# Block 0's pass and products moved into the stretch between the steps, and the output blocks' roots taken on GpSimd as a power, with their steps three slots apart

## Chip, cores and metric

The program runs on one core of one Trainium2 chip. The metric is device time in microseconds. Engines are called PE (TensorE), DVE (VectorE), ACT (ScalarE), POOL (GpSimd) and SP (the queue of SyncE that starts most DMAs); L12 is line 12 of the kernel before the change.

## What is computed

Two layers on 2708 nodes with 256 features. The first is a graph layer with a residual and a layer norm. The second makes two propagation steps, over the normalised adjacency R and over an attention A that keeps, in each row of a softmax, the largest entries up to a mass of 0.9.

```python
x = _layernorm(x + relu(concat([x, adj @ x]) @ weight + bias))
R = adj + eye;  R = R / R.sum(-1, keepdims=True)
Z, Xf, Xa = 0, x, x
for n in range(2):
    A = top_p_attention(Xa, W1, W2, W3)      # softmax, nucleus of 0.9, renormalised
    Xf = R @ Xf
    Xa = A @ Xa
    Z = Z + Xf @ U1[n].T + Xa @ U2[n].T
h = x + Z
x = _layernorm(x + _layernorm(h) * ln_g + ln_b)
```

(`adj` is the second layer's S too. A layer norm divides by the root of the variance plus 1e-5.)

## The kernel before

The nodes are cut into 22 blocks of 128 rows, the last with 20. The first layer runs to about 285 us. Then come the two attention steps; the change touches the border between them and all of the second.

**Step 2 as a pipeline.** A loop `for per in range(NB + 2)` (L1271) has periods, each cut into six slots `g`. What is issued in a slot stands in each engine's queue in the order of the code, and every engine works its queue in that order. In period `per` four blocks are under way:

- block `per + 2` (`b_exp`): logits on PE (L507, in three parts, with one PSUM buffer), `shift` on DVE (L841, the row maximum of an excerpt), Exp on ACT (`exps2`, L844 and L848), and at the end `begin_search` on DVE (L852 to L857);
- block `per + 1` (`b_act`): a search for the threshold in whole passes over the row on ACT (`try_act`: L965, Relu with a sum; L968, Sign with a sum; small steps L971 to L981);
- blocks `per` and `per - 1`: on DVE (`vector_slots`), the one gets `last_level`, `below_level` (L1022) and `candidates` (L1029), the other `in_order` (L1038, L1041), `threshold`, `mark` (L1082) and `mask` (L1087), which sets what is dropped to zero;
- block `t_mul = per - 2`: `turn` (PE transposes four 128 x 128 blocks, L527; ACT copies them to `wT`, L530 and L533) and `products` (L564, one slot later), six groups for 22 blocks.

Blocks 0 to 2 are started ahead of the loop: their logits and Exp end beside `ya_pair` (L672 on PE, copies L675 on ACT), which makes the right side of the products. DVE searches block 0 by two passes (`try_dve`, L992), and ACT makes one more (`try_act(b0, 1, 0)`, after all of the `ya_pair`s). The spill of ACT's passes is the upper half of `tile2`, in the room of `xaT_all`, which the `ya_pair`s read.

**R's products.** R has few entries per row, so for a block m of R only the needed rows are fetched: seven indirect DMAs on POOL (`y_load`, L719), and two loads of R's values and one of own rows on SP. Eight matmul steps ("units", `r_units`, L749) make the product. `y_load` of block m + 1 is issued with the first unit of m and needs the buffer of m - 1. A table `units` says how many units a period issues: 8, 8, then 18 in periods 2 to 9, none in 10, and 16 from 11 on (two blocks of R: their first units are in slots 0 and 3). In slot 0 units stand ahead of the first `turn`, in the others behind it.

**Output blocks.** When a block has its product with A and its second with R (`arrive`, L792), it goes to `ready`. A `Final` then gets two layer norms, one a period: `load` of x1 (SP, L1176), `stats` (DVE, L1181 and L1182), `roots` (ACT, Sqrt, L1217), `over` (DVE, reciprocal L1220 and L1221), then `end` for blocks at their second norm and `middle` for those at their first: both apply the norm on ACT (L1191), `middle` also scales and adds on POOL (L1206, L1207), and `store` (SP, L1214). `final_slot` spreads them: `over`, `end` and `middle` in slot 0, `store` in 1, `load` in 2, `stats` in 3, `roots` in 5. In the last period (`tail`) the norm is applied on DVE, and after the loop `roots` and `over` are called three times more for what is left.

Of the kernel before, what the change touches and what calls it, by code (L numbers as in the profile page):

```python
# [9 lines left out]
FP = mybir.dt.float32  # L10
I32 = mybir.dt.int32
AF = mybir.ActivationFunctionType  # L12
ALU = mybir.AluOpType
# [5 lines left out]
LN_EPS = 1e-5  # L19

P = 128
# [19 lines left out]
CW, CC = 128, 7  # L41
# [107 lines left out]
def fast_path(ctx, tc, c, flags, fint, xT_d, x_d, w0_d, b0_d, w1_d, w2_d, w3_d, u1_d, u2_d, g_d, b_d):  # L149
    nc = tc.nc  # L150
# [3 lines left out]
    NW = SEG * NS  # L154
# [344 lines left out]
    def logits(s, t, i):  # L499


        p = rows(t)
        lg = ps_lg()
        cs = CHS[2 * i:2 * i + 2]
        for h, (a, b) in enumerate(cs):
            o = slice(DA * h, DA * h + DA)
            nc.tensor.matmul(lg[:p, h, :b - a], lhsT=q[o, t * P:t * P + p], rhs=keys[s][o, i, :b - a],  # L507
                             start=True, stop=True)
        a, b = cs[0][0], cs[-1][1]
        return lg.rearrange("p h n -> p (h n)")[:p, :b - a], a, b  # L510
# [151 lines left out]
    def ya_pair():  # L662


        if not y_pairs:
            return
        t0 = y_pairs.pop(0)
        pz = ps_acc().rearrange("p (s d) -> p s d", d=D)
        for s in range(2):
            p, at = rows(t0 + s), (t0 + s) * P  # L670
            for j in range(DC):
                nc.tensor.matmul(pz[:p, s, :], lhsT=xaT_all[:, j, at:at + p], rhs=c.u2[:, j, 1, :],  # L672
                                 start=j == 0, stop=j == DC - 1)
        if rows(t0 + 1) == P:
            nc.scalar.copy(ya[:, t0:t0 + 2, :], pz)  # L675
            return
        for s in range(2):
            nc.scalar.copy(ya[:rows(t0 + s), t0 + s, :], pz[:rows(t0 + s), s, :])
# [129 lines left out]
    def e2(t):  # L808
        return ring[t % 5]
# [40 lines left out]
    def begin_search(b):  # L850

        nc.vector.tensor_reduce(b.z, b.all[:b.p, :NL], AX.X, ALU.add)  # L852
        yield
        nc.vector.reciprocal(b.rz, b.z)
        nc.vector.tensor_scalar(b.nz, b.z, -1.0, None, op0=ALU.mult)
        yield
        nc.vector.tensor_scalar(b.l0, b.roots, b.roots, b.rz, op0=ALU.mult, op1=ALU.mult)  # L857

    def run_all(steps):
        for _ in steps:  # L860
            pass
# [84 lines left out]
    for t in range(3):  # L946
        exps2(blocks[t], 2, *logits(1, t, 2))
        ya_pair()
    while y_pairs:
        ya_pair()  # L950

    tile1 = big.tile([P, 2 * NW], FP, tag="x1", name="w")
    low = tile1[:, :NW]
    w = tile1[:, NW:]
    tile2 = big.tile([P, 2 * NW], FP, tag="V", name="e4")
    nc.gpsimd.memset(tile2[:, N:NW], 0.0)
    ring.append(tile2[:, :NW])
    scr = tile2[:, NW:]

    def try_act(b, k, part):  # L960


        e = e2(b.t)[:b.p, :N]
        if part == 0:
            nc.scalar.activation(scr[:b.p, :N], e, AF.Relu, bias=b.nz, scale=b.l[k], accum_out=b.relu)  # L965
            return
        if part == 1:
            nc.scalar.activation(scr[:b.p, :N], e, AF.Sign, bias=b.nz, scale=b.l[k], accum_out=b.sign)  # L968
            return
        if part == 2:  # L970
            nc.scalar.activation(b.n, b.sign, AF.Identity, bias=halfn[:b.p], scale=0.5)  # L971
            return
        nc.scalar.activation(b.u[k], b.relu, AF.Identity, bias=b.n, scale=b.rz)
        next_level(b, k)

    def next_level(b, k):
        keep, slope, down = STEPS[k]
        nc.scalar.activation(b.kept, b.l[k], AF.Copy, scale=keep + TOP_P * slope, bias=-down)
        nc.scalar.activation((b.l1, b.l2)[k], b.u[k], AF.Identity, bias=b.kept, scale=-slope)
        if k:  # L980
            nc.scalar.activation(b.few, b.l1, AF.Copy, scale=TOP_P, bias=-FEW)  # L981
# [6 lines left out]
    def try_dve(b, k):  # L988

        e = e2(b.t)[:b.p, :N]  # L990
        level(b, b.l[k])
        nc.vector.scalar_tensor_tensor(w[:b.p, :N], e, b.d, e, op0=ALU.is_ge, op1=ALU.mult, accum_out=b.m)  # L992
        nc.vector.tensor_scalar(b.u[k], b.m, b.rz, b.l[k], op0=ALU.mult, op1=ALU.mult)
        if k == 0:
            keep, slope, down = STEPS[0]
            nc.vector.tensor_scalar(b.kept, b.l0, keep + TOP_P * slope, -down, op0=ALU.mult, op1=ALU.add)
            nc.vector.scalar_tensor_tensor(b.l1, b.u0, -slope, b.kept, op0=ALU.mult, op1=ALU.add)
# [165 lines left out]
    sds = small.tile([P, 8], FP, tag="sds", name="sds", bufs=1)  # L1163
    nbs = small.tile([P, 8], FP, tag="nbs", name="nbs", bufs=1)
    nc.gpsimd.memset(mvs, 1.0)

    class Final:

# [45 lines left out]
            nc.sync.dma_start(out=out_d[t * P:t * P + p, :], in_=self.h[:p])  # L1214

    def roots(a, b):
        nc.scalar.activation(sds[:, a:b], mvs[:, a:b, 1], AF.Sqrt, bias=c.eps, scale=1.0)  # L1217

    def over(a, b):
        nc.vector.reciprocal(sds[:, a:b], sds[:, a:b])  # L1220
        nc.vector.scalar_tensor_tensor(nbs[:, a:b], mvs[:, a:b, 0], -1.0, sds[:, a:b], op0=ALU.mult, op1=ALU.mult)  # L1221

    def final_slot(i):


        if i == 2:
            while ready and len(new) < 2:
                new.append(Final(*ready.pop(0)))
                new[-1].load()
        if i == 1:  # L1230
            while done:
                done.pop().store()
        n = len(new) + len(finals)
        if i == 3:
            for k, f in enumerate(new + finals):
                f.stats(k)
        if i == 5 and n:
            roots(0, n)
        if i == 0 and n:
            over(0, n)  # L1240
            for f in finals:
                f.end()
            for f in new:
                f.middle()
            done[:] = finals
            finals[:] = new
            new.clear()

    accs = {}


    each = NB * (CC + 1)
    first = 2 * (CC + 1)
    units = {0: CC + 1, 1: CC + 1}
    rest = each - first - sum(units.values())
    units.update({p: rest * (p - 1) // 8 - rest * (p - 2) // 8 for p in range(2, 10)})
    units.update({p: each * (p - 10) // 11 - each * (p - 11) // 11 for p in range(11, 22)})
    assert first + sum(units.values()) == 2 * each

# [1 line left out]
    b0, b1, b2 = (blocks[t] for t in range(3))  # L1261
    run_all(begin_search(b0))
    try_dve(b0, 0)
    run_all(begin_search(b1))
    try_dve(b0, 1)
    run_all(begin_search(b2))
    lg = logits(1, 3, 0)
    r_units(first)
    try_act(b0, 1, 0)
    next_level(b0, 1)  # L1270
    for per in range(NB + 2):  # L1271
        if per == NB + 1:
            tail.append(True)
        n_r = units.get(per, 0)
        b_act = blocks.get(per + 1)
        t_mul = per - 2 if per > 1 else None
        if t_mul is not None:
            accs[t_mul] = ps_acc(t_mul)
        b_exp = None
        if per and per + 2 < NB:  # L1280
            b_exp = blocks[per + 2] = Block(per + 2)
        vector = vector_slots(blocks.get(per), blocks.get(per - 1), begin_search(b_exp) if b_exp else None)
        for g in range(NG):
            n = n_r * (g + 1) // NG - n_r * g // NG
            now = later.pop(0)
            later.append([])
            if g == 0:
                if b_exp:
                    shift(b_exp, lg[0])
                r_units(n)  # L1290
            if t_mul == EDGE:
                if g == 0:
                    products(0)
                    edge_product(ya, accs[EDGE], e2(EDGE))
            elif t_mul is not None:
                turn(t_mul, g, ya, accs[t_mul], e2(t_mul))
            if b_exp and g == 3:
                lg = logits(1, b_exp.t, 2)
            if g == NG - 1 and 3 < per + 3 < NB:
                lg = logits(1, per + 3, 0)  # L1300
            if g:
                r_units(n)
            if b_exp and g == 1:
                lg = logits(1, b_exp.t, 1)
            if t_mul is not None and t_mul != EDGE:
                products(1)
            if b_exp and g in (0, 1, 3):
                exps2(b_exp, (g + 1) // 2, *lg)
            if b_act:
                for k, part in {0: ((0, 0),), 1: ((0, 1), (0, 2), (0, 3)), 2: ((1, 0),), 3: ((1, 1), (1, 2), (1, 3))}.get(g, ()):  # L1310
                    try_act(b_act, k, part)
            next(vector)
            if g == 0:
                final_slot(0)
                if t_mul:
                    t = t_mul - 1
                    base = za_load(t)
                    later[0].append(lambda t=t, base=base: arrive(t, base, accs.pop(t), ras.pop(t)[:rows(t)]))
            for f in now:
                f()  # L1320
            if g and (per < NB + 1 or g < NG - 1):
                final_slot(g)
    t = EDGE
    base = za_load(t)
# [405 lines left out]
```

## Time and profile before

| | us |
|---|---|
| three runs | 1323.46, 1325.51, 1327.99 (median 1325.51) |
| profiled execution, device time | 1323.33 |
| its span, first to last instruction | 1321.6 |
| PE busy in it | 1237.4 (94%) |
| DVE busy | 1002.0 (76%) |
| ACT busy | 753.3 (57%) |
| POOL busy | 634.7 (48%) |

The profile is of one execution. Its span leaves out 1.7 us around the program. Shares of the whole span mix stages: before 285 us PE is nearly alone, afterwards all engines work at once. "Idle before" in a row tells how long an engine stood still and what ended that; idle time of an engine that others do not wait for costs nothing.

Step 2 begins with the last `ya_pair` near 754 us and ends with the span. The masks (L1087) of blocks 0 and 1 start at 777.32 and 807.62; then they come 24.17 us apart up to block 8, and from block 12 to 18 about 26.65 us apart.

### The profile page before, as it was taken

The page shows a single profiled execution, that of the slowest core. Times are in us where ns is not written, and L with a number is a line of the kernel's source. Part 1 is how long each engine was busy: PE and PEld are TensorE (multiplying, and loading weights), DVE is VectorE, ACT ScalarE, POOL GpSimd, SP SyncE. Part 2 cuts the span into 40 slices and gives each one's busy share as a digit, 9 for nine tenths or more (in the row PEclk, how much of TensorE's full clock was granted, in tenths as well). Part 3 has the DMA queues.
Part 4 walks back from the last instruction along what each step waited for, and adds up shares of the span by engine and source line. Part 5 has one row for each costly group of instructions (what it writes and reads, how often), then busy time and mean ns, then how long its engine had stood idle before and what let it go on. Part 6 is the DMA issues. An engine that isn't in the chain of part 4 may idle for free.

```text
span 1321.6 us, 18910 instructions
## 1 busy us (share of the span) xinstructions
PE 1237.4 (94%) x5764; PEld 894.5 (68%) x5764; DVE 1002.0 (76%) x3420; ACT 753.3 (57%) x1338; POOL 634.7 (48%) x594
## 2 busy tenths in 40 slices
PE   8999999979899999999999969999999989998985
PEld 6877877833477777777775647777756766666763
DVE  2545555865999998877751399898897999899996
ACT  2010111025465556566564498878888899989931
POOL 1000000005275532677554187887847767787850
PEclk9999999989899999999998979999999999999998
DMA  7455544523222210223232155556545445544541
GB/s 191 163 173 168 167 153 142 171 67 123 92 77 82 70 62 10 76 91 99 76 77 86 55 172 179 177 178 184 172 118 159 148 128 166 173 148 146 166 108 38
DMA packets 101994, 166.28 MB, mean 126 GB/s; under 512 B 17394, under 2 KB 74358, under 8 KB 101882
## 3 DMA queue, kind: packets, MB, share of 16 engines
q1 hardware_dynamic: 75596, 108.91, 25.4%
q0 software_dynamic: 20544, 51.17, 14.1%
q10 hardware_dynamic: 5742, 4.89, 1.3%
q8 instruction: 48, 0.79, 0.2%
q14 instruction: 64, 0.52, 0.1%
HBM read 130.87 MB, written 34.03 MB: 125 GB/s over the span
## 4 chain that ended last, share of the span: by engine, by line
PE 70%; ACT 15%; DVE 11%; issue 3%; DMA 0%; ACTq 0%; DVEq 0%
PE acc L564 23%; PE acc L257 16%; PE lg L507 8%; PE tr L527 6%; PE misc L749 5%; ACT e L965 4%; ACT e L844 3%; ACT e L968 2%; DVE e L1087 2%; PE acc L651 2%; PE acc L462 2%; PE misc L426 2%; PE misc L392 2%; ACT e L848 2%; PE acc L672 2%
## 5 line engine op out<-in xcount | busy, mean ns | idle before, releaser
L530 ACT COPY wT<-tr 128x512 f32<-128x512 f32 (+2 forms) x258 | 131.8, 518 | 217.6 <-PE tr L527 215.9
L564 PE MATMUL acc<-ya,wT 128*128 128x256 f32 (+1 forms) x924 | 234.9, 394 | 11.4 <-ACT wT L530 11.0
L564 PE MATMUL acc<-x,wT 128*128 128x256 f32 (+1 forms) x924 | 230.5, 388 | 0.0
L719 POOL DMA_INDIRECT yg<-v_d,ix x154 | 195.0, 1266 | 64.6 <-issue 25.1
L564 PEld LDWEIGHTS acc<-ya,wT 128*128 128x128 f32 (+1 forms) x924 | 171.4, 194 | 66.0 <-issue 23.1
L719 POOL DMA_INDIRECT yg<-yf_d,ix x154 | 190.7, 1238 | 48.3 <-issue 24.3
L564 PEld LDWEIGHTS acc<-x,wT 128*128 128x128 f32 (+1 forms) x924 | 165.2, 189 | 71.0 <-issue 37.3
L257 PE MATMUL acc<-y,adj_t 128*128 128x257 f32 (+1 forms) x924 | 208.4, 381 | 0.0
L257 PEld LDWEIGHTS acc<-y,adj_t 128*128 128x128 f32 (+1 forms) x924 | 171.8, 189 | 32.7 <-issue 8.9
L367 POOL DMA_INDIRECT adj_t<-in_adj,ix x154 | 165.6, 1076 | 51.8 <-issue 41.7
L749 PE MATMUL misc<-yg,adj_t 128*128 128x256 f32 (+1 forms) x704 | 180.6, 392 | 5.9 <-DMA yg<-yf_d,ix 4.3
L507 PE MATMUL lg<-k,q 64*128 64x512 f32 (+3 forms) x528 | 152.4, 605 | 29.7 <-ACT e L848 22.3
L749 PEld LDWEIGHTS misc<-yg,adj_t 128*128 128x128 f32 (+1 forms) x704 | 125.2, 190 | 54.3 <-issue 23.1
L527 PE MATMUL tr<-ident,e 128*128 128x128 f32 (+2 forms) x946 | 147.9, 275 | 2.5 <-DVE e L1087 2.5
L527 PEld LDWEIGHTS tr<-ident,e 128*128 128x128 f32 (+2 forms) x946 | 114.1, 140 | 41.9 <-issue 18.8
L334 POOL DMA_DIRECT2D part_d<-e x1 | 0.6, 573 | 285.3 <-DVE e L333 285.3
L439 ACT COPY x1T<-tr 128x256 f32<-128x256 f32 (+1 forms) x22 | 8.0, 364 | 186.7 <-PE tr L438 186.7
L965 ACT ACTIVATE e<-e,st 128x2708 f32<-128x2708 f32 (+1 forms) x43 | 113.5, 2640 | 0.1
L968 ACT ACTIVATE e<-e,st 128x2708 f32<-128x2708 f32 (+1 forms) x42 | 111.0, 2642 | 0.1
L570 DVE MAX8 cand<-e 128x8 f32<-128x170 f32 (+1 forms) x352 | 87.2, 317 | 27.4 <-ACT e L514 27.4
L1029 DVE MAX8 cand<-w 128x8 f32<-128x136 f32 (+1 forms) x440 | 106.1, 285 | 0.0
L507 PEld LDWEIGHTS lg<-k,q 64*128 64x128 f32 (+1 forms) x528 | 39.5, 184 | 63.5 <-ACT e L848 30.1
(239 smaller groups left out, 1780.8 us busy)
## 6 DMA issues: line engine op xcount, KB each, us to landing
adj_t<-in_adj SPq DMA_DIRECT2D x44, 704.0 KB
adj_t<-adjc_d SPq DMA_DIRECT2D x44, 448.0 KB
adjc_d<-adj_t SPq DMA_DIRECT2D x22, 256.0 KB
base<-za_d SPq DMA_DIRECT2D x41, 128.0 KB
adjc_d<-adj_t SPq DMA_DIRECT2D x22, 192.0 KB
xt<-in_x ACTq DMA_DIRECT2D x21, 128.0 KB
x_d<-x SPq DMA_DIRECT2D x21, 128.0 KB
x1b_d<-xb SPq DMA_DIRECT2D x21, 128.0 KB
```

The costliest lines, as they stand in the source:

```text
L257: nc.tensor.matmul(acc[:p, :n], lhsT=halves[k // KH][:kw, k % KH, :p], rhs=y[:kw, k, :n], start=k == 0, stop=stop and k == NB - 1)
L367: nc.gpsimd.indirect_dma_start(out=a[:CW, i, :], out_offset=None, in_=adj_rows, in_offset=bass.IndirectOffsetOnAxis(ap=ix[:CW, m, i:i + 1] ...
L507: nc.tensor.matmul(lg[:p, h, :b - a], lhsT=q[o, t * P:t * P + p], rhs=keys[s][o, i, :b - a], start=True, stop=True)
L527: nc.tensor.transpose(tr[:kw, k % 4, :p], e[:p, k * P:k * P + kw], ident[:p, :p])
L530: nc.scalar.copy(wT[:, :full, :p], tr[:, :full, :p])
L564: nc.tensor.matmul(acc[:p, :D], lhsT=wT[:kw, k % 4, :p], rhs=y[:kw, k, :], start=k == 0, stop=k == NB - 1)
L570: nc.vector.max(dst[:p, i * 8:(i + 1) * 8], src[:p, i * step:i * step + w])
L719: nc.gpsimd.indirect_dma_start(out=y[:CW, i, :], out_offset=None, in_=rows_d, in_offset=bass.IndirectOffsetOnAxis(ap=ix[:CW, m, i:i + 1], ...
L749: nc.tensor.matmul(acc[:p, :D], lhsT=a[:kw, k, :p], rhs=y[:kw, k, :], start=k == 0, stop=k == CC)
L965: nc.scalar.activation(scr[:b.p, :N], e, AF.Relu, bias=b.nz, scale=b.l[k], accum_out=b.relu)
L968: nc.scalar.activation(scr[:b.p, :N], e, AF.Sign, bias=b.nz, scale=b.l[k], accum_out=b.sign)
L1029: nc.vector.max(b.cand[:p, 8 * i:8 * i + 8], low[:p, SEG2 * i:SEG2 * (i + 1)])
```

## The change

It has two parts.

*Block 0.* ACT's pass over block 0 is issued after the third of the `ya_pair`s that follow the Exps, ahead of the remaining ones, and spills into `low` (the lower half of the tile whose upper half is `w`) until `tile2` is there. `next_level(b0, 1)` follows DVE's second pass. Block 0 is transposed and multiplied in slots 4 and 5 of period 1, three groups in each, and no longer in period 2. Period 2 issues 20 units of R, periods 3 to 9 share the other 124 (17 or 18 each).

*Output blocks.* `roots` runs on GpSimd, as an addition of 1e-5 and a power of -0.5, and `over` loses the reciprocal. `over`, `end` and `middle` move from slot 0 to slot 2, `store` and `load` to slot 3, `stats` from slot 3 to slot 5, ahead of `roots`. In the last period `roots` is left to the calls after the loop.

```diff
     for t in range(3):
         exps2(blocks[t], 2, *logits(1, t, 2))
         ya_pair()
-    while y_pairs:
-        ya_pair()
...
-    tile2 = big.tile([P, 2 * NW], FP, tag="V", name="e4")
-    nc.gpsimd.memset(tile2[:, N:NW], 0.0)
-    ring.append(tile2[:, :NW])
-    scr = tile2[:, NW:]
+    spill_room = [low]
...
+        scr = spill_room[0]
...
+    power = small.tile([P, 8], FP, tag="power", name="power", bufs=1)
+    nc.gpsimd.memset(power, -0.5)
...
     def roots(a, b):
-        nc.scalar.activation(sds[:, a:b], mvs[:, a:b, 1], AF.Sqrt, bias=c.eps, scale=1.0)
+        nc.gpsimd.tensor_scalar(sds[:, a:b], mvs[:, a:b, 1], LN_EPS, None, op0=ALU.add)
+        nc.gpsimd.tensor_tensor(sds[:, a:b], sds[:, a:b], power[:, a:b], op=ALU.pow)
 
     def over(a, b):
-        nc.vector.reciprocal(sds[:, a:b], sds[:, a:b])
         nc.vector.scalar_tensor_tensor(nbs[:, a:b], mvs[:, a:b, 0], -1.0, sds[:, a:b], op0=ALU.mult, op1=ALU.mult)
 
     def final_slot(i):
-        if i == 2:
-            while ready and len(new) < 2:
-                new.append(Final(*ready.pop(0)))
-                new[-1].load()
-        if i == 1:
-            while done:
-                done.pop().store()
         n = len(new) + len(finals)
-        if i == 3:
-            for k, f in enumerate(new + finals):
-                f.stats(k)
-        if i == 5 and n:
-            roots(0, n)
-        if i == 0 and n:
+        if i == 2 and n:
             over(0, n)
             for f in finals:
                 f.end()
...
+        if i == 3:
+            while done:
+                done.pop().store()
+            while ready and len(new) < 2:
+                new.append(Final(*ready.pop(0)))
+                new[-1].load()
+        if i == 5:
+            for k, f in enumerate(new + finals):
+                f.stats(k)
+            if n and not tail:
+                roots(0, n)
...
-    units = {0: CC + 1, 1: CC + 1}
+    units = {0: CC + 1, 1: CC + 1, 2: 20}
...
-    units.update({p: rest * (p - 1) // 8 - rest * (p - 2) // 8 for p in range(2, 10)})
+    units.update({p: rest * (p - 2) // 7 - rest * (p - 3) // 7 for p in range(3, 10)})
...
     try_dve(b0, 0)
+    try_act(b0, 1, 0)
+    while y_pairs:
+        ya_pair()
     run_all(begin_search(b1))
     try_dve(b0, 1)
+    next_level(b0, 1)
     run_all(begin_search(b2))
+    tile2 = big.tile([P, 2 * NW], FP, tag="V", name="e4")
+    nc.gpsimd.memset(tile2[:, N:NW], 0.0)
+    ring.append(tile2[:, :NW])
+    spill_room[0] = tile2[:, NW:]
     lg = logits(1, 3, 0)
     r_units(first)
-    try_act(b0, 1, 0)
-    next_level(b0, 1)
...
-        t_mul = per - 2 if per > 1 else None
+        t_mul = 0 if per == 1 else per - 2 if per > 2 else None
...
-            elif t_mul is not None:
+            elif t_mul:
                 turn(t_mul, g, ya, accs[t_mul], e2(t_mul))
             if b_exp and g == 3:
                 lg = logits(1, b_exp.t, 2)
+            if t_mul == 0 and g > 3:
+                for i in range(3):
+                    turn(0, 3 * (g - 4) + i, ya, accs[0], e2(0))
+                    products(1)
             if g == NG - 1 and 3 < per + 3 < NB:
                 lg = logits(1, per + 3, 0)
             if g:
                 r_units(n)
...
-            if t_mul is not None and t_mul != EDGE:
+            if t_mul and t_mul != EDGE:
                 products(1)
...
             if g == 0:
-                final_slot(0)
                 if t_mul:
                     t = t_mul - 1
                     base = za_load(t)
...
-            if g and (per < NB + 1 or g < NG - 1):
+            if g:
                 final_slot(g)
```

## The prediction, made before the change was built

> **What bounds the kernel now.** I read the stretches first, engine by engine, then the timelines of two places, and last the groups and DMA issues for prices. After the window's length each row of stretches has the busy time of PE, PEld, DVE, ACT and POOL, the granted TensorE clock and the DMA share.
>
> ```profile
> 776.00:800.00 24.00, 17.05 (x69) 11.44 (x70) 23.69 (x83) 21.43 (x32) 19.49 (x15) 0.86 0.43 134
> 800.00:824.00 24.00, 23.69 (x115) 17.84 (x114) 23.19 (x89) 19.75 (x34) 19.06 (x17) 1.00 0.64 195
> 1160.85:1187.50 26.65, 23.80 (x112) 16.97 (x110) 24.25 (x87) 24.85 (x41) 21.04 (x18) 1.00 0.50 158
> ```
>
> Three regimes. Between the steps (776 to 800) DVE and ACT are full and PE has 7 us spare. From period 2 to 9 PE is full (23.69 of 24); a period takes 24.17 us, the spacing of the masks (L1087). From period 13 on, where finished output blocks are normalised too, a period takes 26.65 us and ACT is fullest. Here the chain of waits passes through ACT's searches, the mask and the output norms.
>
> Between the steps:
>
> ```profile
> 784.68 2.08 PE L507 MATMUL lg<-k,q 64*128 64x512 f32 x4 [5.17 <-ACT e L844]
> 789.38 0.28 DVE L841 TENSOR_REDUCE nmax<-lg 128x1 f32<-128x128 f32 x1
> 807.62 3.04 DVE L1087 SCALAR_TENSOR_TENSOR e<-w,st,e 128x2720 f32<-128x2720 f32 x1
> 814.29 0.60 PE L527 MATMUL tr<-ident,e 128*128 128x128 f32 x4
> ```
>
> Period 2 of DVE and ACT begins with L841, which needs the logits L507 of block 4. The mask of block 1 comes 18.2 us later and ends at 810.66; its first transposes are at 814.29, when PE is free. So period 2 has 3.6 us in hand on DVE and none on PE.
>
> In the late regime:
>
> ```profile
> 1101.09 3.04 DVE L1087 SCALAR_TENSOR_TENSOR e<-w,st,e 128x2720 f32<-128x2720 f32 x1
> 1101.57 3.37 POOL L719 DMA_INDIRECT yg<-v_d,ix  x1 [0.30 <-PE tr L527]
> 1104.45 1.28 ACT L1217 ACT_TABLE_LOAD   x1
> 1106.01 1.03 PE L749 MATMUL misc<-yg,adj_t 128*128 128x256 f32 x4
> 1107.57 0.58 ACT L530 COPY wT<-tr 128x512 f32<-128x512 f32 x1 [1.52 <-PE tr L527]
> 1108.16 1.28 ACT L844 ACT_TABLE_LOAD   x1
> 1114.60 1.08 ACT L1191 ACTIVATE yg<-yg,nbs,sds 128x256 f32<-128x256 f32 x2
> 1116.25 0.73 POOL L1206 TENSOR_TENSOR yg<-yg,gb 128x256 f32<-128x256 f32 x1 [1.34 <-ACT yg L1191]
> 1119.43 0.99 POOL L719 DMA_INDIRECT yg<-v_d,ix  x1
> ```
>
> Call the first copy of a period T (here 1107.57). ACT works without a gap from T to T+22.63 (end of slot 3), copies twice more, PE multiplies, does two R units and transposes, and the next T is at 26.65. The load for Exp lies in this loop; the load for Sqrt lies before ACT's wait of 1.52 us, outside it. A gather that meets a mask on DVE ends 0.81 us after the mask (1104.94) and not after 0.95.
>
> **Part 1, block 0.** ACT's pass over block 0 (L965) now starts at 754.30, after the last ya copies. It moves to the end of the third in-loop copy, 748.48 + 0.59 = 749.07, and takes 2.65 + 0.18. Three ya copies stand behind it; PE's two accumulators let the last pair begin only after the first of these (752.4), so it ends near 754.2, its copies at 754.9, the level steps (0.19 + 0.30 + 0.19) at 755.6. Block 1's pass was at 757.45, so ACT gains about 1.7 us; PE's first R units come 0.6 us later, behind which POOL's gathers wait by as much, uncritically.
>
> The products cost more. Slots 4 and 5 of period 1 now issue 22 transposes, six copies and five of six product groups, and these stand on PE's queue **ahead of the logits for block 4**. The copies are behind ACT's slot 3, which ends at 788.5, then at 786.8. Five groups at 2.17 us each (spacing of transposes 991.37 to 993.54), one R unit 0.5, the logits 1.06: 786.8 + 0.6 + 10.85 + 0.5 + 1.06 = 799.8. The clock of 0.86 says that one group runs at half rate, 3.24 us for 1.89 (row of 1288.23), so 801.1. L841 was at 789.38 and is 11.7 us late; behind it on DVE is the whole of period 2, behind that ACT's Exp. The mask starts 18.0 us after L841 (18.24, less the 0.67 that DVE waited there), lasts 3.05, and block 1's transposes come at 822.2 instead of 814.29: **7.9 us later**. PE idles meanwhile: 20 R units at 0.49 (1.46 for three) and logits fill 13 of 21 us. Two units more in period 2 leave two fewer later, -1.0. Part 1: **+6.9** (+4 if the clock is full and the 1.7 larger, +10 if the half clock returns).
>
> **Part 2, roots on GpSimd.** Removed per late period: two loads, 2 x 1.283 (groups view: 8 under L1217, 7 under L844), Sqrt 0.30, a reciprocal 0.15 on DVE. Worth on the path: only the load at L844, so ACT's loop falls from 26.65 to 25.37. The other 1.58 us widen a wait; they count only if PE came sooner. DVE does 26.65 - 2.12 (its wait for L844) - 0.15 = 24.4 us per period, so that is the floor beneath.
>
> The Trainium skill ("ScalarE: Activation LUTs", What ACT_TABLE_LOAD costs) gives 1.28 us plus a drain of 1.38 for a switch. The trace has 1.283 and the next instruction 0.02 us on (1104.45 + 1.28, then Sqrt at 1105.75). With the drain, seven periods would give 9.7 us more; I go by the row.
>
> Added on POOL: an add and a power on 128 x 4. Neither is in the trace. Bounds: 0.11 (memset of 128 x 16) and 1.16 (L369, 128 x 128); the add is near L358 (128 x 7, 0.26), for the power I take 0.5. Before POOL's next gathers that is 0.8, between 0.2 and 2.3.
>
> Moved: over, end and middle to slot 2, stores and loads to slot 3, statistics to slot 5. On ACT this moves four L1191 (1.97) within the loop: nothing. On DVE 2.16 us of statistics move behind the mask, covered by its wait. On SP the store waits until T+16.2 with only the next period's loads behind it: nothing. **On POOL it is not free.** L1206 ran at T+8.68. L965 of slot 2 ends at T+17.5, less 1.28 and 1.97 is T+14.2; the third L1191 releases POOL 1.65 later (1114.60 to 1116.25), T+15.87; four operations take 3.18 to the next gather: T+19.05, against T+11.86. Seven gathers queue behind, whose rows PE needs for two units *before* the next T. And the mask, at T+20.17 before, starts at T+18.89, so the first gather meets it: it ends at 18.89 + 3.04 + 0.81 = 22.74, the second starts at 23.04 and lands after the time of the DMA view:
>
> ```profile
> yg<-yf_d,ix POOLq DMA_INDIRECT x154, 3.3
> yg<-v_d,ix POOLq DMA_INDIRECT x154, 3.8
> ```
>
> That is 26.3 to 26.8. From the second R unit to the next copy are 1.13 us (four L749 in 1.03 from 1106.01, so the second unit starts near 1106.44, to 1107.57): period 27.5 to 28.0, I take **27.7, not 25.37**. Should the first gather slip in before the mask, 26.4. Seven periods (13 to 19) at +1.05: **+7.3**; ends -9.0 (25.37) and +18 (29.2: rows landing 1.5 us later, as at 768.20, where PE got one 4.3 us after its gather of 762.96 had ended).
>
> The Trainium skill ("SBUF — State Buffer", Who interferes with whom) holds that a DVE operation with two SBUF inputs takes only the shared read interface, so writing descriptors goes on. The trace has gathers of 3.37 us beside exactly such an operation. By that sentence the second gather starts at T+20.3 and lands at T+24.1, and the period would be ACT's 25.37; I go by the rows.
>
> Periods 20 to 22 are DVE's (23.4 us): 0. Tail: statistics to nbs takes 0.57 us now (1308.49 to 1309.06) and 0.94 with add and power; once or twice on the path: +0.4 (-0.3 to +3.5).
>
> **Sum.** 6.9 + 7.3 + 0.4 = +14.6. The profiled execution took 1323.33 (span 1321.6), hence 1338; the median shown is 2.2 above it, so I say 1339.
>
> **Rivals.** *ACT's loop decides the late periods*: gathers land in time, 25.37, so 6.9 - 9.0 + 0.4 = -1.7: 1323, no change. For it: the gather that starts at 1092.78 is used at 1106.01, some 9 us after landing. Against: 7.2 of these go by the move, 2.7 by the mask, 1.3 by the faster loop. *All of ACT's relief counts* (the other side): if PE reaches T sooner too, the period falls to DVE's 24.4, seven times -2.25 is -15.7, total -8.4: 1316; it decides for faster below 25.1 per period. Against: ACT waits 1.52 us at T already. *Period 2 is short*: without products it lasts PE's 13.3 us, not DVE's 21, part 1 is -1.0 and the sum +6.7: 1331. Against: DVE is 23.69 of 24 busy there. *The power is dear*: at 3 us per call POOL's cycle (14 gathers at 1.25, two held by 2.4, 3.18, 3.0) is 28.5 and `over` is late on DVE; with the wait for rows some 29.4, 1.7 more a period: 1350.
>
> **Chances.** Forecast 0.60 (own range 1330 to 1347), ACT's loop 0.15, all relief 0.10, short period 2 0.10, dear power 0.05. A change under 0.3% (4 us) can't be told from none: faster 0.11, within 0.14, slower 0.75. The range leaves out the 1316 and 1323 cases in part: 1324 to 1350.
>
> **What would show it.** Masks of blocks 0 and 1 about 43 us apart (30.3 now), L841 of block 4 near 801 with DVE idle before it; one Exp load left and none per period; late masks 27.7 apart, with L749 in slot 0 waiting for yg<-v_d and a gather of 3.4 us just behind L1207. Late masks at 25.4 and no such wait would prove part 2 wrong; a spacing of 33 there, part 1.

## The result, and the profile after

After takes **1341.45 us** (median of four executions, 1340.16 to 1345.64) where before took 1324.59 (median of four): ratio 1.0124, 95% interval 1.0105 to 1.0144. Its profiled execution has a span of 1339.1 us, before's had 1321.6. The change costs 17 us, on both sides of the middle of step 2: between the steps, and where finished blocks are normalised.

The stretches of after that answer to the three shown of before (window, length; then busy time of PE, PEld, DVE, ACT and POOL, each with its number of instructions; granted clock, DMA share, GB/s). The third is again one late period, from first copy to first copy:

```profile
776.00:800.00 24.00, 14.82 (x69) 11.42 (x68) 12.95 (x38) 15.12 (x26) 15.66 (x13) 0.79 0.35 103
800.00:824.00 24.00, 20.62 (x76) 13.19 (x75) 21.48 (x81) 17.45 (x28) 16.85 (x13) 0.86 0.52 153
1170.17:1197.41 27.24, 24.30 (x112) 16.82 (x110) 23.05 (x86) 21.89 (x37) 21.87 (x21) 1.00 0.50 153
```

In after's code the mask is L1083, the norm L1189, scale and add L1204 and L1205, add and power of the roots L1215 and L1216; L507, L530, L564, L719, L749 and L841 are where they were. Between the steps DVE was full before (23.69 of 24) and now does 12.95: it stands still for nearly half of the time. In the late period ACT fell from 24.85 to 21.89, so its relief is real and larger than the one load on its loop, and yet the period grew from 26.65 to 27.24. No engine is busy all through it; it is a chain of waits.

Between the steps, from the timeline of after (start, length, engine, line, operation, the tiles written and read; in brackets the idle time before it and what ended it):

```profile
788.79 3.60 PE L564 MATMUL acc<-ya,wT 128*128 128x256 f32 x8 [7.49 <-ACT wT L530]
801.20 1.13 PE L507 MATMUL lg<-k,q 64*128 64x512 f32 x4
802.38 0.29 DVE L841 TENSOR_REDUCE nmax<-lg 128x1 f32<-128x128 f32 x1 [13.15 <-PE lg L507]
819.88 3.04 DVE L1083 SCALAR_TENSOR_TENSOR e<-w,st,e 128x2720 f32<-128x2720 f32 x1
823.28 0.60 PE L527 MATMUL tr<-ident,e 128*128 128x128 f32 x4
```

The first product group of block 0 runs at half rate (3.60 us, 1.89 for the later ones; the granted clock is 0.54 during the first and 1.00 from 792 to 801), the logits of block 4 come only at 801.20, and DVE has waited 13.15 us for them. Block 1's mask starts 42.8 us after block 0's, 30.3 before.

A late period of after:

```profile
1174.66 0.25 POOL L1215 TENSOR_SCALAR sds<-mvs 128x4 f32<-128x4 f32 x1
1174.99 1.04 POOL L1216 TENSOR_TENSOR sds<-sds,power 128x4 f32<-128x4 f32 x1
1184.29 1.08 ACT L1189 ACTIVATE yg<-yg,nbs,sds 128x256 f32<-128x256 f32 x2
1185.94 0.72 POOL L1204 TENSOR_TENSOR yg<-yg,gb 128x256 f32<-128x256 f32 x1 [1.10 <-ACT yg L1189]
1188.94 3.04 DVE L1083 SCALAR_TENSOR_TENSOR e<-w,st,e 128x2720 f32<-128x2720 f32 x1
1189.11 3.74 POOL L719 DMA_INDIRECT yg<-v_d,ix  x1
1193.15 0.95 POOL L719 DMA_INDIRECT yg<-v_d,ix  x1 [0.31 <-issue]
1196.18 0.30 PEld L749 LDWEIGHTS misc<-yg,adj_t 128*128 128x128 f32 x2 [0.54 <-DMA yg<-v_d,ix]
1197.41 0.58 ACT L530 COPY wT<-tr 128x512 f32<-128x512 f32 x1 [5.13 <-PE tr L527]
```

Read it as a chain: ACT's norm (1184.29) releases POOL's scale and add, behind these stands the first gather, it meets the mask (1188.94) and takes 3.74 us instead of 0.95, the second gather's rows land 3.0 us after its start, PE uses them at 1196.18, then transposes, and ACT's first copy ends 5.13 us of idling.

The starts of the mask operation give the whole account. Distances of masks in us; "0 to 10" is from block 0's mask to block 10's, "late" the mean of the six distances from 12 to 18, "end" from the last mask to the end of the span. The last six rows are of experiments below: four that ran where no other waits disturb them, and two (with figures in brackets) of which only the part from block 10 on is compared:

| kernel | 0 to 10 | 11 to 12 | late | 18 to 19 | 19 to 20 | 20 to 21 | end |
|---|---|---|---|---|---|---|---|
| before | 248.1 | 25.69 | 26.64 | 23.46 | 23.37 | 15.66 | 24.8 |
| after | 255.2 | 24.28 | 27.28 | 24.22 | 27.71 | 16.47 | 27.1 |
| e11_after_here | 255.2 | 24.28 | 27.15 | 24.22 | 27.82 | 17.51 | 25.5 |
| e12_block0_again | 255.3 | 25.69 | 26.64 | 23.47 | 23.36 | 15.66 | 26.8 |
| e9_free_scale_add | 248.4 | 24.28 | 25.24 | 23.33 | 22.72 | 17.58 | 27.2 |
| e10_end_on_vector | 248.2 | 24.29 | 24.64 | 24.29 | 23.77 | 15.83 | 25.9 |
| e8_early_table | (265.6) | 24.28 | 25.26 | 23.46 | 23.42 | 15.66 | 26.9 |
| e5_power_old_slots | (264.3) | 24.29 | 25.26 | 25.63 | 25.60 | 15.39 | 26.7 |

### The profile page after: what moved, and what is told of

Read it like the earlier page. It is cut to its first block, busy times and chain, and to the rows that moved or that the text cites. A ratio compares the mean times of both kernels' runs of the same rounds, so it can differ in the third digit from the quotient of the medians.

```text
span 1339.1 us, 18886 instructions
## 1 busy us (share of the span) xinstructions
PE 1246.3 (93%) x5764; PEld 895.0 (67%) x5764; DVE 993.4 (74%) x3406; ACT 729.8 (55%) x1309; POOL 659.4 (49%) x623
## 3 DMA queue, kind: packets, MB, share of 16 engines
q1 hardware_dynamic: 75596, 108.91, 25.5%
## 4 chain that ended last, share of the span: by engine, by line
PE 73%; ACT 16%; DVE 4%; issue 3%; DMA 3%; POOL 1%; ACTq 0%; POOLq 0%; DVEq 0%
PE acc L564 25%; PE acc L257 15%; PE lg L507 8%; PE misc L749 7%; PE tr L527 6%; ACT e L961 3%; ACT e L844 3%; ACT e L964 2%; PE acc L651 2%; ACT e L848 2%; DMA yg<-v_d,ix 2%; ACT wT L530 2%; PE acc L462 2%; PE misc L392 2%; PE misc L426 2%
## 5 line engine op out<-in xcount | busy, mean ns | idle before, releaser
L530 ACT COPY wT<-tr 128x512 f32<-128x512 f32 (+2 forms) x258 | 131.9, 519 | 255.5 <-PE tr L527 253.6
L564 PE MATMUL acc<-ya,wT 128*128 128x256 f32 (+1 forms) x924 | 233.1, 392 | 16.1 <-ACT wT L530 15.9
L564 PE MATMUL acc<-x,wT 128*128 128x256 f32 (+1 forms) x924 | 230.5, 388 | 0.0
L719 POOL DMA_INDIRECT yg<-v_d,ix x154 | 193.5, 1256 | 60.4 <-issue 29.7
L719 POOL DMA_INDIRECT yg<-yf_d,ix x154 | 191.3, 1242 | 55.9 <-issue 23.4
L564 PEld LDWEIGHTS acc<-ya,wT 128*128 128x128 f32 (+1 forms) x924 | 171.5, 194 | 66.3 <-ACT wT L530 24.9
L749 PE MATMUL misc<-yg,adj_t 128*128 128x256 f32 (+1 forms) x704 | 189.1, 401 | 25.8 <-DMA yg<-v_d,ix 4.9
L564 PEld LDWEIGHTS acc<-x,wT 128*128 128x128 f32 (+1 forms) x924 | 165.3, 190 | 70.9 <-issue 37.3
L749 PEld LDWEIGHTS misc<-yg,adj_t 128*128 128x128 f32 (+1 forms) x704 | 124.1, 192 | 85.2 <-issue 28.2
L507 PE MATMUL lg<-k,q 64*128 64x512 f32 (+3 forms) x528 | 151.4, 601 | 14.9 <-ACT e L848 9.8
L570 DVE MAX8 cand<-e 128x8 f32<-128x170 f32 (+1 forms) x352 | 87.2, 317 | 26.7 <-ACT e L514 26.7
L1078 DVE MATCH_REPLACE8 w<-part,e 128x680 f32<-128x680 f32 (+1 forms) x88 | 74.3, 850 | 0.0
```

The source lines that it names most:

```text
L530: nc.scalar.copy(wT[:, :full, :p], tr[:, :full, :p])
L564: nc.tensor.matmul(acc[:p, :D], lhsT=wT[:kw, k % 4, :p], rhs=y[:kw, k, :], start=k == 0, stop=k == NB - 1)
L570: nc.vector.max(dst[:p, i * 8:(i + 1) * 8], src[:p, i * step:i * step + w])
L719: nc.gpsimd.indirect_dma_start(out=y[:CW, i, :], out_offset=None, in_=rows_d, in_offset=bass.IndirectOffsetOnAxis(ap=ix[:CW, m, i:i + 1], ...
L749: nc.tensor.matmul(acc[:p, :D], lhsT=a[:kw, k, :p], rhs=y[:kw, k, :], start=k == 0, stop=k == CC)
```

## The experiments

The first eight kernels ran on two other chips, on which before itself takes 1382 (e1 to e4) and 1372 us (e5 to e8), with more scatter. There the engines stand for 1 to 13 us at many places for which the trace names no releaser, most of them before block 10 (the figures in brackets above): e1 to e8 have 25 to 39 idle times over 1 us marked "issue" on PE, DVE and ACT ahead of block 10's mask, before and e9 to e12 have one. Part of the marks are waits whose event is missing: DVE's wait of 2.12 us for ACT's Exp in before's late periods is "issue" in e1. What lies behind the others is open. Absolute times in the expectations are therefore read as distances from before, and sizes from the late masks: kernels with before's output steps have 26.64 there too, to 0.01 us. The last four ran where before takes 1323.2 and 1324.5.

**Block 0 alone, and which part of it.** e1 has block 0's changes with before's output steps. e3 keeps only the early pass of ACT. e4 is e1 with two lines more and one condition changed:

```diff
+            if per == 1 and g == 4:
+                lg = logits(1, per + 3, 0)
             if t_mul == 0 and g > 3:
                 for i in range(3):
                     turn(0, 3 * (g - 4) + i, ya, accs[0], e2(0))
                     products(1)
-            if g == NG - 1 and 3 < per + 3 < NB:
+            if g == NG - 1 and per > 1 and per + 3 < NB:
```

> Part 1 alone (block 0 sooner), output steps as before. Theory (products of block 0 stand ahead of block 4's logits on PE, so L841 is late): L841 of block 4 at about 802, masks 0 to 1 about 43 us apart, block 1's mask 12 later than before, the time 6 to 9 us above before: 1331 to 1333. Rival (the loss lies in the output steps, block 0's delay is caught up in periods 2 to 9): masks 0 to 1 also 43, but the end at 1323 to 1326.

> Of part 1 only the early ACT pass over block 0; its products stay in period 2, units as before, output steps as before. Theory (the products are the whole loss of part 1; the 1.7 us that ACT gains are waited away for logits): 1322 to 1325, masks 0 to 1 about 30 apart. Rival (the pass in the other buffer delays something by itself): 1328 or more.

> Part 1 alone as in e1_block0, but the logits of block 4 are issued ahead of block 0's transposes and products in slot 4 of period 1. Theory (what costs is only the place of the logits on PE's queue, and DVE's search of period 2 does not need the later Exp): L841 of block 4 at 789 to 791, masks 0 to 1 about 31 apart, 1320 to 1326. Rival 1 (ACT's six copies of block 0, paced by PE, stand ahead of the Exp of block 4 on ACT, and the delay of 9 to 12 us only moves to period 3): masks 0 to 1 about 31, 1 to 2 some 33, and 1330 to 1333 as in e1_block0. Rival 2 (products in PE's idle time are a gain once nothing waits behind them): 1312 to 1318.

Against before: e1 1.0097 (1.0064 to 1.0130), e3 1.0027 (0.9996 to 1.0057), e4 1.0074 (1.0042 to 1.0106). e3 can't be told from no change, and its masks 0 to 1 are 29.6 apart: no cost of the pass is seen (its interval leaves room for up to 8 us on that chip), and the loss points to the products. e1's 13 us were above what the theory gave, and its masks 0 to 1 were 35.5 apart and not 43: block 0's own mask came late there (821.27), and L841 waited 5.51 us for the logits, not 13. That size stayed open until e12.

e4 is the telling one. L841 starts 12.06 us after block 0's mask, exactly as in before and in e3, so DVE's wait for the logits is gone. But the mask of block 1 still comes 34.9 us after block 0's. The waits of e4 from 814 to 880 (total, times, longest), and its timeline:

```profile
DVE bulk L852 <- ACT e L844: 6.4, 1, 6.4
```

```profile
823.50 0.58 ACT L530 COPY wT<-tr 128x512 f32<-128x512 f32 x1 [3.61 <-PE tr L527]
826.25 0.28 DVE L841 TENSOR_REDUCE nmax<-lg 128x1 f32<-128x128 f32 x1
828.27 0.59 ACT L530 COPY wT<-tr 128x512 f32<-128x512 f32 x1 [1.58 <-PE tr L527]
830.53 1.10 ACT L844 ACTIVATE e<-lg,nmax 128x1024 f32<-128x1024 f32 x1
```

DVE has its logits at 826.25, but ACT's Exp of the same block waits for 4.3 us more behind copies that PE's transposes pace, and DVE later waits 6.4 us for the block's last Exp (for 2.6 of them ACT itself waits, and the trace names no engine for it). This is the mechanism of rival 1, that moving the logits forward moves the wait from DVE to ACT, though its figures are not met: the 5.3 us beyond e3 are lost in period 2 itself (29.6 to 34.9), not in the next.

**Block 0 alone once more**, the same kernel as e1:

> Part 1 alone once more, since e1_block0 ran where the kernel before took 1382 us with waits that no event explains. Theory (block 0's products cost what after's masks show): masks 0 to 1 42.8 apart, mask 10 some 6.8 later than before, late masks at 26.65, the time 6 to 8 us above before, 1329 to 1332. Rival (part 1 alone costs more than within after, as e1_block0 had it): 12 us or more above before.

1332.38 against 1324.49 us: 1.0059 (1.0045 to 1.0073), +7.9. From its timeline (logits L507 at 803.40):

```profile
804.58 0.29 DVE L841 TENSOR_REDUCE nmax<-lg 128x1 f32<-128x128 f32 x1 [13.24 <-PE lg L507]
```

The same wait as in after, masks 0 to 1 at 42.88, and from 0 to 10 it takes 255.3 us as after does. Part 1 costs 7 to 8 us, and its 7 us in the masks lie before block 10.

**The output steps alone.** e2 is before with all of the diff's changes to Final, `roots`, `over` and `final_slot`.

> Part 2 alone (roots as a power on GpSimd, steps three slots apart), block 0 as before. Theory (POOL's scale and add wait in slot 2 and hold the gathers behind them): late masks 27.2 to 27.7 apart (26.65 before), gathers of 3.7 us just behind L1207's successor, the time 7 to 10 us above before: 1332 to 1335. Rival (ACT's loop decides and all of after's loss is block 0's): late masks 25.4 apart, 1314 to 1318.

1.0052 (1.0020 to 1.0084), 7 us. Late masks 27.27 apart on the mean, 27.40 from 19 to 20: after's figures without block 0's part. From block 10's mask to the end e2 takes 306.3 us, before 296.1. The theory of the move holds; ACT's loop alone does not decide.

**Move or power?** e5 has the power on GpSimd in the old slots, e6 the new slots with Sqrt and reciprocal:

```diff
 # e5, against before
-        nc.scalar.activation(sds[:, a:b], mvs[:, a:b, 1], AF.Sqrt, bias=c.eps, scale=1.0)
+        nc.gpsimd.tensor_scalar(sds[:, a:b], mvs[:, a:b, 1], LN_EPS, None, op0=ALU.add)
+        nc.gpsimd.tensor_tensor(sds[:, a:b], sds[:, a:b], power[:, a:b], op=ALU.pow)
...
-        nc.vector.reciprocal(sds[:, a:b], sds[:, a:b])
 # e6, against e2
-        nc.gpsimd.tensor_scalar(sds[:, a:b], mvs[:, a:b, 1], LN_EPS, None, op0=ALU.add)
-        nc.gpsimd.tensor_tensor(sds[:, a:b], sds[:, a:b], power[:, a:b], op=ALU.pow)
+        nc.scalar.activation(sds[:, a:b], mvs[:, a:b, 1], AF.Sqrt, bias=c.eps, scale=1.0)
...
+        nc.vector.reciprocal(sds[:, a:b], sds[:, a:b])
```

> The roots as a power on GpSimd, but each step in its old slot (statistics 3, roots 5, the rest 0); all else as before. Theory of the move (the loss comes from scale and add standing in slot 2): the late masks are closer than before's 26.65, 25.4 if ACT's loop decides alone. Theory of POOL's own cycle (14 gathers at 1.25, two of them held 2.4 longer by DVE, scale and add 3.0, together 25.3, and now add and power 1.6 to 1.8 more): late masks 26.9 to 27.2 apart and the time 2 to 4 us above before. The two differ by 1.5 us per period, 10 us in all.

> The output steps in after's slots (statistics 5, over, end and scale and add 2), but with Sqrt on ACT and the reciprocal on DVE; all else as before. Theory of the move: the chain from ACT's norm in slot 2 over POOL's scale and add and the two gathers to the first copy stays, and the load for Exp comes back into it: late masks 28.3 to 28.7 apart, the time 15 to 20 us above before. Theory of POOL's own cycle (the power's 1.6 us are what after loses): late masks at 26.65 or below, the time 0 to 3 us above before.

e5: **0.9951** (0.9922 to 0.9980), late masks 25.26 apart. e6: 1.0121 (1.0067 to 1.0175), late masks 29.03 apart on the mean (28.45 to 30.05). Both go against POOL's own cycle as the bound: with the power POOL keeps up with 25.26, and without it the new slots are the slowest of all. That cycle was counted too long, since how often and for how long DVE holds a gather is not fixed. POOL has nothing in hand in e5, though: from mask 12 to mask 19 it never pauses for more than 0.31 us (busy for 20.9 to 21.3 us of each 25.3, the rest are pauses of 0.2 to 0.3 between its operations). e5 also shows where the power does cost. In the last periods, which are short (23.4 us in before), its masks are 25.6 apart:

```profile
1300.26 1.05 POOL L1220 TENSOR_TENSOR sds<-sds,power 128x4 f32<-128x4 f32 x1
1301.34 0.16 DVE L1223 SCALAR_TENSOR_TENSOR nbs<-mvs,sds 128x4 f32<-128x4 f32 x1 [1.99 <-POOL sds L1220]
```

In the old slots `over` is the first thing on DVE in a period, and there DVE waits 1.99 us for the power.

**Taking the wait away.** e7 leaves POOL's scale and add out; e9 keeps them in place, on tiles that are always ready. The outputs of both lack scale and add:

```diff
 # e7, against e2
-            nc.gpsimd.tensor_tensor(h[:p], h[:p], c.gb[:p, 0, :], op=ALU.mult)
-            nc.gpsimd.tensor_tensor(h[:p], h[:p], self.x1[:p], op=ALU.add)
...
 # e9, in their place
+            nc.gpsimd.tensor_tensor(still[:p, 0], c.gb[:p, 0, :], c.gb[:p, 0, :], op=ALU.mult)
+            nc.gpsimd.tensor_tensor(still[:p, 0], c.gb[:p, 0, :], c.gb[:p, 1, :], op=ALU.add)
```

> As e2_outputs, but GpSimd's scale and add of the middle step (four operations per period) are left out in all periods but the last, so that no gather stands behind ACT's norm; the outputs lack them. Theory of the move: the wait of PE for yg<-v_d in slot 0 goes, late masks 25.2 to 25.6 apart, the time 5 to 9 us below before. Rival (something else of the new order holds the period, the statistics behind the mask or the power): late masks stay at 26.6 or more.

> As e2_outputs, with GpSimd's four operations of the middle step kept in their place and length, but on tiles that are always ready (gains and biases into a tile that nobody reads), so that they wait for no norm of ACT; the middle step's outputs lack scale and add. Theory (the wait of POOL for ACT's norm in slot 2, with the gathers behind it, is the loss): late masks 25.2 to 25.7 apart. Rival (the sheer work of POOL, add and power among it, is the loss): 26.9 to 27.3 as in e2_outputs.

e7 came out slower than before, 1.0132 (1.0087 to 1.0176), against the expectation. Its late masks are of two kinds: two of six 25.25 apart, as the theory has it, the others 27.9 to 32.1. In a long one:

```profile
1173.15 0.58 ACT L530 COPY wT<-tr 128x512 f32<-128x512 f32 x1 [2.56 <-issue]
```

ACT stands for 2.56 us with no event that releases it ("issue"), though the transposes that it copies ended at 1168.81, and PE and DVE stand with it. The copy starts 0.13 us after the last of twelve gathers that follow each other every 1.25 us. Whether these hold it is open; the trace shows no wait for rows there. e9 has POOL's work at its full length and ran undisturbed: all late masks are 25.20 to 25.26 apart, ratio 0.9959 (0.9944 to 0.9974). From its timeline:

```profile
1170.28 0.73 POOL L1210 TENSOR_TENSOR still<-gb 128x256 f32<-128x256 f32 x1
1171.16 0.98 POOL L719 DMA_INDIRECT yg<-v_d,ix  x1 [0.15 <-issue]
1175.12 3.04 DVE L1087 SCALAR_TENSOR_TENSOR e<-w,st,e 128x2720 f32<-128x2720 f32 x1
1181.59 0.58 ACT L530 COPY wT<-tr 128x512 f32<-128x512 f32 x1 [3.13 <-PE tr L527]
```

The gathers start 4 us ahead of the mask, not behind it, and ACT's wait at its first copy falls from 5.1 to 3.1 us. Same slots, same power, same length on POOL: what is missing is the wait for ACT's norm, and with it go 2 us per late period, and the stretch from mask 19 to 20 falls from e2's 27.40 to 22.72. (DVE's statistics no longer read POOL's results either; in after DVE waits for these only behind masks 19 and 20, 0.8 us each.) PE's weight loads wait for rows of a gather 17 times between 1080 and 1245 us in after, and not once in e9 between 1080 and 1220. For these periods the theory is shown.

**A better version.** Of all that part 2 removes, only the load of Exp's table was on ACT's loop. e8 is before with one column of Exp behind Sqrt, which fetches the table in ACT's wait; e10 besides moves the last norm to DVE:

```diff
         nc.scalar.activation(sds[:, a:b], mvs[:, a:b, 1], AF.Sqrt, bias=c.eps, scale=1.0)
+        if not tail:
+            nc.scalar.activation(early, c.eps, AF.Exp)
...
 # e10 besides, in Final.end
-            self.norm(self.h)
+            i, p, h = self.i, self.p, self.h
+            nc.vector.tensor_scalar(h[:p], h[:p], sds[:p, i:i + 1], nbs[:p, i:i + 1], op0=ALU.mult, op1=ALU.add)
```

> Before with one operation added: directly behind Sqrt in slot 5 ACT takes the Exp of a single column, so that the table for Exp is loaded in ACT's wait ahead of its first copy and not behind it. Theory (of part 2 only this load lay in ACT's loop, and 1.28 + 0.2 us fit into the wait of 1.52): late masks 25.3 to 25.5 apart, 8 to 9 us below before. Rival 1 (POOL's cycle, 25.3 without its wait, grows by a gather that meets another DVE operation): 26.0 to 26.5, 1 to 4 us below before. Rival 2 (PE's rows or transposes set the period, ACT's load is covered): 26.65, no change.

> As e8_early_table (Exp's table fetched behind Sqrt), and the last norm of the two finished blocks on DVE instead of ACT. ACT's loop loses 1.0 us per period, DVE's 23.7 busy grows by about 0.7. Theory (the loop through ACT still ends last at 25.26): late masks 24.3 to 24.7 apart, 12 to 16 us below before. Rival (DVE becomes the bound at once, its work does not fit without gaps): 25.2 or more, no better than e8_early_table.

e8: 0.9961 (0.9930 to 0.9993), late masks 25.26 apart as expected, and nothing lost from mask 18 to 21. That is 5 us where 8 to 9 were expected; the interval covers 1 to 10, and in the profiled execution the last product of PE took 5.47 us for before's 3.30 (see the tail below). Its ACT at the turn of a period:

```profile
1176.92 1.28 ACT L1218 ACT_TABLE_LOAD   x1
1178.22 0.30 ACT L1218 ACTIVATE sds<-mvs,eps 128x4 f32<-128x4 f32 x1
1178.53 1.28 ACT L1220 ACT_TABLE_LOAD   x1
1179.83 0.20 ACT L1220 ACTIVATE early<-eps 128x1 f32<-128x1 f32 x1
1180.03 0.59 ACT L530 COPY wT<-tr 128x512 f32<-128x512 f32 x1
```

Both loads now lie ahead of the first copy, where ACT would have waited anyway. e10 takes **1312.34 us** against 1323.17: 0.9921 (0.9907 to 0.9934), the best of all kernels here. Its late masks are 24.64 apart, with DVE and ACT equally full; one stretch of 25 us:

```profile
1155.00:1180.00 25.00, 24.25 (x117) 17.76 (x117) 24.65 (x90) 24.71 (x42) 20.66 (x19) 1.00 0.54 169
```

The expected 12 to 16 us were not quite reached (10.8): the periods from mask 18 on took 0.8 and 0.4 us more, and in the profiled execution the last product 1.7.

**After on the last chip:**

> After itself, on the chip of these runs. If the two parts are independent, its late masks are 27.0 to 27.5 apart as in e2_outputs, and its distance to before is that of e1_block0 and e2_outputs together, 15 to 22 us; if one part covers the other, it is no more than the larger of the two, 13.

1342.08 us, 1.0145 (1.0130 to 1.0161), +18.9. Beside e12's +7.9 that leaves 11 for part 2, which was not run alone on these chips; e2 has 7 (3 to 12). By the masks, which the other chips leave alone from block 10 on, the parts add up: e12's 7.1 up to block 10 and e2's 10.2 from there on are 17.3, after has 17.5 and e11 16.2.

## Why the prediction was right, and where its steps were not

The predicted time was 1339, 1341.45 was measured, and both mechanisms of the forecast are the ones that the runs show. In its sum one term was far too large and two were too small. (A slip besides: 14.6 on the profiled 1323.33 and 2.2 more for the median are 1340, not 1339.)

**Block 0 (+6.9): right.** Predicted L841 at 801.1, measured 802.38; block 1's transposes 822.2, measured 823.28; masks 0 to 1 43, measured 42.8; net cost at block 10's mask 255.18 - 248.14 = +7.0. The 1.1 to 1.3 us that everything came later are mostly the 1.7 that ACT should have gained: block 1's pass did start sooner (754.80 for 757.45), but PE's logits then came late for ACT, and the copies that were due at 786.8 started at 788.18. From L841 to the mask 18.0 us were taken; the stated difference, 18.24 - 0.67, is 17.57, and 17.50 was measured. The "-1.0 for two fewer units" is not seen in that form: of the 9.0 us that block 2's mask was late, 0.5 are won back until block 9 and 1.7 from mask 9 to 10. There before's PE ran one product group in 3.16 us and after's in 2.00, at a granted clock of 0.61 and 1.00, so 1.2 of the 1.7 are the clock.

**Late period (27.7): right, with one term too large.** Relative to the first copy T (1170.17): norm T+14.2 predicted, T+14.12 measured; scale T+15.87, measured T+15.77; first gather T+19.05, measured T+18.94; its end T+22.74, measured T+22.68; second start T+23.04, measured T+22.98. PE then had the rows 2.8 to 3.3 us after that start, not 3.3 to 3.8, so the period is 27.28 and not 27.7.

**"Seven periods at +1.05: +7.3": wrong.** The first of them, mask 11 to 12, gained 1.4 (24.28 for 25.69): the first scale and add come at 1076.9, so a gather meets a mask behind them only from mask 12 (1079.86) on, and up to there ACT's shorter loop counts. The other six cost 0.65 each, +3.9. Together +2.5. e8 and e9, whose gathers are never late, have the same 24.28 there.

**"Periods 20 to 22 are DVE's: 0": the step that failed.** They cost 0.76, 4.34 and 0.81, +5.9. The sum was made as if a period that DVE sets could not be set by late rows. From after's timeline:

```profile
1254.10 0.58 ACT L530 COPY wT<-tr 128x512 f32<-128x512 f32 x1 [7.18 <-PE tr L527]
1266.03 1.07 ACT L1189 ACTIVATE yg<-h,nbs,sds 128x256 f32<-128x256 f32 x2
1267.98 3.53 POOL L1204 TENSOR_TENSOR yg<-yg,gb 128x256 f32<-128x256 f32 x1
1282.35 0.58 ACT L530 COPY wT<-tr 128x512 f32<-128x512 f32 x1 [10.10 <-PE tr L527]
```

ACT's wait at its first copy grows from 5.1 to 7.2 and 10.1 us. In the first of these periods it is the chain from the norm again: POOL waits 1.05 us for it, and the gather behind meets the mask (3.71 us). In the second, which costs the 4.34, POOL does not wait for the norm. That ends at 1267.10, and the scale starts at 1267.98, straight behind a gather. POOL's queue is late by itself: from 1240.58 to 1299.9 it never pauses for more than 0.31 us, and DVE holds two gathers (3.71 and 3.73 us) and then the scale (3.53 for 0.72). So the next gathers start only at 1273.95, and PE's two R units ahead of that copy run at 1278.15 and 1280.18, the latter after a wait for rows. The amount of POOL's work is not enough to explain it: e9 has the same operations, its queue enters these periods 4 us ahead of the mask, and it takes 22.72 from mask 19 to 20. Nor is the power: e6, without it, has 27.55, e2 27.40. So it is the move again, here through a lateness of POOL's queue that a short period leaves no room to recover; that last link is read from the rows and was not tested by itself.

**Power (0.5) and add (0.26).** Measured 1.04 and 0.25. The half microsecond too little did not count, because POOL waited 1.10 us for ACT's norm behind the power anyway. The rival of a dear power is out; so is "all of ACT's relief", since with no late rows the period is 25.24, the 25.37 of "ACT's loop", and not 24.4.

**Tail (+0.4).** It was 2.3 us longer in after and 0.7 in e11. The difference between the two is the last product of PE, of after and then of e11:

```profile
1317.88 4.90 PE L550 MATMUL acc<-ya,wT 128*20 128x256 f32 x44 [0.65 <-ACT wT L546]
```

```profile
1318.16 3.30 PE L550 MATMUL acc<-ya,wT 128*20 128x256 f32 x44 [0.65 <-ACT wT L546]
```

The same kernel, 1.6 us apart, at a granted clock of 0.67 and 1.00. Before had 3.30 too, e12 with before's output steps 5.66 at 0.57. Without that product the end takes 21.49 us in before, 22.20 in after and 22.21 in e11: the change itself costs 0.7 at the end.

**Sum.** +7.0 + 2.5 + 5.9 + 2.3, less 0.2 before block 0's mask, is the 17.5 us between the spans, where 14.6 was forecast. One term was 5 too large, another 6 too small and the tail 2, of which 1.6 are the slow last product of that one execution. That the time fell so close owes something to luck.

## What to carry to other kernels

An operation that waits takes along whatever stands behind it on its queue: before moving it three slots, list what follows it there, and who needs that soonest. What that costs differs from regime to regime (0.65 us in a period of 26.6, 4.3 in one of 23.4), so price it in each, not only in the one that it was found in. And where an engine has a wait in every turn of a loop, look for work of its own that can be pulled into it; here one column of Exp brought 1.4 us per period, and the removal of both table loads brought no more.

## What the runs showed of the hardware

- A gather on POOL that meets the two-input mask of DVE took 3.74 us instead of 0.95, in after and in e6, and ended 0.9 us after the mask; POOL's own two-input scale took 3.53 instead of 0.72 beside a mask.
- A power on 128x4 took 1.04 us on POOL, 0.89 on 128x3, four times an add (0.25).
- After a table load the next operation of ACT starts 0.02 us later (1176.92 + 1.28, then 1178.22) where it waits for no data, twice in a row. The Trainium skill ("ScalarE: Activation LUTs", What ACT_TABLE_LOAD costs) counts a drain of 1.38 us with each; no run here shows one, and e8's ACT, busy for 24.97 of 25.26 us, has no room for two.
- On two of the chips before took 3.7 to 4.4% longer (1372 and 1382 us). In the kernels traced there (e1 to e8) the engines stand at many places ahead of block 10, while the late periods of those with before's output steps (e1, e3, e4) agree with before's to 0.01 us.
